# Edge-gated graph kernel: gates ahead of the products in the last nine blocks, early loads moved to GpSimd, and other steps for the row products

## The chip, the cores and the metric

The kernel runs on one core of a Trainium2 chip. The metric is device time in microseconds (us) of one launch; lower is better. Engines are named as in the profile: PE is TensorE (PEld its weight loads), DVE is VectorE, ACT is ScalarE, POOL is GpSimd, SP is SyncE, which here only issues DMAs. Each engine runs its own instructions strictly in the order in which the program lists them; engines wait for each other, and for DMAs, through semaphores.

## The reference

Sixteen graphs share one adjacency matrix `adj` of 1024 x 1024, with some 9 nonzero entries a row. Each of the 1024 nodes has a row of 256 features for each graph. Cut to what matters:

```python
pre_u  = einsum('bud,dk->buk', h, W1[:256])
pre_v  = einsum('bvd,dk->bvk', h, W1[256:])
hidden = relu(pre_u[:, :, None, :] + pre_v[:, None, :, :] + b1)
S   = sigmoid(einsum('buvk,ko->buvo', hidden, W2)[..., 0] + b2)   # a gate for each pair of nodes
a_t = einsum('buv,bud->bvd', S * adj, h)                          # gated sum over neighbours
m_t = einsum('uv,bud->bvd', adj, h) * h                           # plain sum, times h
out = beta1 * h + beta2 * (a_t @ Wa + ba) + beta3 * (m_t @ Wm + bm)
```

A gate is needed only where `adj` is nonzero. The kernel therefore works on a list of edges and never forms the 1024 x 1024 x 256 tensor.

## The kernel before

**Tables, blocks, steps.** The sixteen graphs form four groups of four. For each group there is a table in device memory, with one row for each node: its `pre_u` features for the four graphs and its `h` features for the four graphs (8 KB together). A block is a group with 128 target nodes; there are 32 of them. The first sixteen are six of group 0, six of group 1, then the last two of group 0 and the last two of group 1 (`order`, L408 to L411); the eight of group 2 and the eight of group 3 follow. A block has ten steps (`T`), and a step handles 128 edge slots. Step `n` belongs to block `k = n // 10`, and `s = n % 10` is its place in it; there are 320 steps.

**A step.** `fetch` (L515) is an indirect DMA on POOL that brings the table rows of 128 source nodes into one of eight buffers `fetched`. `expand` (L602) makes `pre_v` of the 128 edges' targets on PE, into one of two PSUM buffers `pc`, from `X`, which holds `pre_v` of the block in split precision. `add` (L637) adds `pc` to `fetched` on DVE. `gate` (L641) is four DVE operations (relu, times W2, sum) with one sum for each graph; then ACT makes the sigmoid (L650) and scales four left-hand matrices by it (L652, tile `left`). `left_adj` (L611) prepares on ACT the left-hand matrices of the next step with the adjacency values. `aggregate` (L655) multiplies `left` by the fetched `h` rows on PE and sums in PSUM (`acc`). When the buffer is used up, the next fetch goes out.

**Products around the steps.** `products` (L800) places the other PE work by step: `halves` makes `X` for the next block (L473: half products at `s` 1 and 3, casts of X on ACT at 4, 6 and 7); `turn_over` (L674) transposes the sums through the PSUM buffers `misc` (there are two) and ACT copies them into `LT` (L685); `block_end` (L701) multiplies `LT` of the block before by `w_a` and `w_m` at `s` 4 to 7, ACT copies each result out of PSUM (L718), and DVE adds it to `h_blk` a step later (L719), from where SP writes it out. `after(step, f)` puts work off to a step, and `do(n)` issues what is due.

**Row products.** The `pre_u` half of the tables is a product too. `rows` (L452) makes it for 128 nodes of a group in two halves: PE multiplies a transposed input tile `hT` by `w_u`, ACT copies the half into a buffer `tab0` or `tab1` (L461, one buffer for each half), and a step later SP writes that buffer to the table (L465). Group 0 is done before step 0 by a `script` (L544), which also builds the first four edge lists. For group 1 the steps are a written plan (L775): for each of its eight tiles the step of the load of `hT` and the steps of the two halves. `made_rows` (L784) carries out the plan, and sends with the load the `h` half of the table (`copy_h`, a DMA on ACT's queue). Table 1 must be complete before step 60 is fetched. The tiles of the plan take two buffers in turn.

**Edge lists.** `lists(vt)` (L242) builds the edge list of 128 target nodes from a row block of `adj`, the key: some sixty small DVE operations, which `fill` slips between the four gate operations of steps. The first four lists are made before step 0. The fifth to eighth start at steps 0, 16, 48 and 88 (`start_list`, L766), first with the key load on POOL (L244), then four steps later with the operations.

**The order within a step.** The order on each engine is written out by hand, in the main loop from L860. Up to step 309: aggregates of earlier steps, `expand(n + 2)`, in step 8 of a block also `do(n)`, then `products(n)`; then `add(n + 1)`, `gate(n)`, `left_adj(n + 1)` and `do(n)`. So ACT has the copies of `products` ahead of the gates of the same step. In the last block the gates come first. At step 1 SP loads `w_a` and `w_m` (L888, L889), which are first used at step 10 (`scale_late`).

Of the kernel before, what the change touches and what calls it, by code (L numbers as in the profile page):

```python
# [13 lines left out]
P = 128  # L14
# [3 lines left out]
def kernel(  # L18
# [42 lines left out]
    nc = tc.nc  # L61
    B, N, D = x.shape
    NT = N // P
    DC = D // P
    GB = 4
# [21 lines left out]
    xT_rows = xT.rearrange("b (c p) n -> p (b c) n", p=P)  # L87
# [6 lines left out]
    def load_weights(src, name, engine=nc.scalar):  # L94
        t = const.tile([P, DC, D], FP, name=name)
        engine.dma_start(t, src.rearrange("(c p) k -> p c k", p=P))
        return t
# [327 lines left out]
        if k in hT_of:  # L425
            hT_free.append(hT_of.pop(k))

    def load_hT(k):
        g, nt = k
        if k in aside_:  # L430
            hTs[k] = hta.tile([P, GB, DC, P], FP, name="hT_")
        else:
            hTs[k] = hT_of[k] = hT_free.pop(0)
        nc.sync.dma_start(hTs[k].rearrange("p b c n -> p (b c) n"),
                          xT_rows[:, g * GB * DC:(g + 1) * GB * DC, nt * P:(nt + 1) * P])

    def copy_h(k, engine=nc.scalar):
        g, nt = k
# [56 lines left out]
    def do(step):  # L495
        for f in due.pop(step, ()):
            f()
# [17 lines left out]
    def fetch(n):  # L515
        k, g, vt, w, j = where(n)
        at_slot[n] = free.pop(0)
        nc.gpsimd.indirect_dma_start(  # L518
            out=fetched[at_slot[n]], out_offset=None, in_=table[g],
            in_offset=bass.IndirectOffsetOnAxis(ap=uidx[:, vt * NW + w, j:j + 1], axis=0),  # L520
            bounds_check=N - 1, oob_is_err=False)
# [19 lines left out]
    for i in range(COPIES):  # L541
        copy_h(turn[i], nc.sync)

    script = ("r r 0 0", "r r 1 0 0", "r r 1", "r 0 0", "r r 1", "0 2 r 1", "0 0 r r", "1 2 r 1", "v r r 2", "r 1 3",  # L544
              "h 2 1 1", "h 2 2 3 u", "2 f 2 2 w h h h", "m 3 w 3 3 3")
    marks, pcs, accs, evs, hbs, LTs, lefts = {}, {}, {}, {}, {}, {}, {}

    def load_mark(q):
# [11 lines left out]
    for t, turns_ in enumerate(script):  # L560
        step = t - 100
        do(step)
        for c in turns_.split():
            if c == "r":
                if m % 2 == 0:
                    piece = rows(turn[m // 2], tabs[m // 2] if m // 2 < len(tabs) else None)
                    next(piece)
                go(piece, step)
                if m % 2 == 0 and m // 2 + COPIES < NT:
                    copy_h(turn[m // 2 + COPIES], nc.sync)  # L570
                m += 1
            elif c == "h":
                go(parts, step)
            elif c == "v":
                fetch_val(T)
                spread(b1_p, b1_b)
                next(parts)
            elif c == "f":
                for n in range(NF):
                    fetch(n)  # L580
            elif c == "u":
                fetch_val(3)
            elif c == "m":
                load_mark(0)
            elif c == "w":
                warm(6)
            else:
                next(made[int(c)], None)
# [174 lines left out]


    advance = {0: (3,), 2: (3,), 4: (3,)}
    start_list = dict(zip((0, 16, 48, 88), range(EARLY, NT)))  # L766
    loads, at = {}, {}

    def plan(blocks, ns):

        for k, (load, *pieces) in zip(blocks, ns):
            loads[load] = k
            at.update((n, k) for n in pieces)

    plan(turn[NT:], ((0, 1, 8), (1, 9, 12), (9, 18, 19), (13, 22, 28), (20, 29, 32), (29, 38, 39), (33, 42, 48), (40, 49, 51)))  # L775
    for g, first in ((2, 60), (3, 140)):
        plan([(g, vt) for vt in range(NT)], ((first - 4 + 10 * i, first + 8 + 10 * i, first + 12 + 10 * i)
                                             for i in range(NT)))
# [4 lines left out]

    def made_rows(n):  # L784
        nonlocal piece, last
        if n in loads:
            if loads[n] in begun and loads[n][0] == 1:
                aside_.remove(loads[n])
            load_hT(loads[n])
            if loads[n] not in begun:  # L790
                copy_h(loads[n])
                begun.add(loads[n])
        if n in at:
            if at[n] != last:
                last = at[n]
                piece = rows(last)
                next(piece)
            go(piece, n)

    def products(n, k, s):  # L800
        nonlocal end, parts
        made_rows(n)
        if (s == 2 and 0 < k < BS) or n == total:
            turn_over(k - 1, 1, 1, n)
        z = 3 if n < ROOM else 4
        if z <= s < z + 4 and 0 < k < BS:
            if s == z:
                end = block_end(k - 1)
                next(end)
            go(end, n)  # L810
        if ROOM <= n < total - T:
            if s in (8, 9):
                turn_over(k, 0, s - 8, n)
        elif s == 7 and k < BS:
            turn_over(k, 0, 0, n)
        if s == 7 and k == BS - 1 or s == 8 and n < ROOM:
            turn_over(k, 0, 1, n)
        if (s == 0 and 0 < k < BS) or n == total - 1:
            turn_over(k - (s == 0), 1, 0, n)
        if n == total - 2:  # L820
            end = tail(tails[:2], n)
            next(end)
        elif n == total - 1:
            go(end, n)
        elif n >= total:
            end = tail([tails[2 + n - total]], n)
            next(end)
            go(end, n)
            go(end, n)
        later = n >= ROOM  # L830
        if k + 1 < BS and s - later in (0, 2, 3, 5, 6):
            if s == later:
                parts = halves(k + 1)
                next(parts)
            go(parts, n)
# [3 lines left out]
    left_adj(0)  # L839
    total = BS * T  # L840
    ROOM, MORE, LISTS = 10, 3, 110
    ahead = NF
    add(0)

# [15 lines left out]
    for n in range(total + 2):  # L860
        k, s = divmod(n, T)
        if n < total - 3:
            last_in = n - 1 if n % 2 or n < ROOM else done
        else:
            last_in = n
        while done < min(last_in, total):
            gather_in(done)
            done += 1
        if n % TW == 1 and n // TW + 1 < total // TW:
            load_mark(n // TW + 1)  # L870
        if n < total - T:
            expand(n + 2)
            if n >= ROOM:
                fill(n, False)
                if s == 8:
                    do(n)
            products(n, k, s)
        if n + 1 < total:
            add(n + 1)
        if n < total:  # L880
            gate(n)
            if n + 1 < total:
                left_adj(n + 1)
        do(n)
        if n >= total - T and n + 2 < total:
            expand(n + 2)
        if n == 1:
            w_a = load_weights(Wa, "w_a", nc.sync)  # L888
            w_m = load_weights(Wm, "w_m", nc.sync)  # L889
            bias = load_rows(bm, D, "bias", nc.sync, spare[:, 1])  # L890
            ba_b = load_rows(ba, D, "ba_b", nc.sync, spare[:, 2])
            be1 = load_rows(beta1, 1, "be1", nc.sync)
            be2 = load_rows(beta2, 1, "be2", nc.sync)
            be3 = load_rows(beta3, 1, "be3", nc.sync)
            after(10, scale_late)
        if s in (5, 7) and k < BS - 1:
            h = s // 7
            hb = big.tile([P, 2, D], FP, name="h_blk", bufs=4)
            hbs.setdefault(k, []).append(hb)
            g, vt = order[k]  # L900
            nc.sync.dma_start(hb.rearrange("p b d -> p (b d)"),
                              table[g][vt * P:(vt + 1) * P, GD + 2 * h * D:GD + (2 * h + 2) * D])
        if n == total - 6:
            hbs[BS - 1] = hT_free.pop(0).rearrange("p b c n -> p b (c n)")
            for v, m, f in tails:
                for h, o in tail_rows(x, v, m, f):
                    nc.sync.dma_start(h, o)
        for i in advance.get(n, ()):
            next(made[i], None)
        if n in start_list:  # L910
            running.append([made[start_list[n]], True, n])
            piece_of(running[-1], n)
        if n < ROOM:
            fill(n, False)
        if n >= total - T:
            products(n, k, s)
        if n == LISTS:
            assert not running and all(next(x, None) is None for x in made)
            lists_done()
            more = main.enter_context(tc.tile_pool(name="more", bufs=1))  # L920
            hT_free.extend(hT_places(more, MORE, NH))
        if n == 120:
            nc.gpsimd.partition_all_reduce(longest, rest, P, bass_isa.ReduceOp.max)
            after(n + 12, count_rest)
# [115 lines left out]
```

## Time and profile before

The median of three runs is 1110.08 us (1110.04 to 1113.46). The profile shows one further execution, of 1097.05 us, and everything from the trace refers to that one.

| | |
|---|---|
| median of the runs | 1110.08 us |
| the profiled execution, its own time | 1097.05 us |
| its span, first to last instruction | 1095.2 us |
| busy: PE, DVE, ACT, POOL | 1029.3, 1020.8, 862.0, 465.5 us |
| DMA | 394.56 MB, 360 GB/s |
| mean granted clock of PE | 0.979 |

By stage, from the trace (busy us of an engine in the stretch):

| stretch, us | what runs | PE | DVE | ACT | POOL | DMA, GB/s |
|---|---|---|---|---|---|---|
| 0 to 60 | group 0 table, four lists | 47.51 | 51.01 | 22.47 | 32.60 | 314 |
| 60 to 160 | first steps, fifth list, group 1 rows | 84.24 | 86.92 | 64.59 | 62.88 | 341 |
| 160 to 360 | the same, sixth and seventh list | 189.80 | 191.01 | 160.70 | 106.58 | 378 |
| 360 to 810 | eighth list, rows of groups 2 and 3 | 444.63 | 430.88 | 386.36 | 177.45 | 391 |
| 810 to 1050 | blocks 23 to 30, no rows any more | 229.57 | 232.06 | 205.79 | 81.81 | 346 |
| 1050 to 1095.2 | last block, tail | 33.59 | 28.91 | 22.09 | 4.15 | 158 |

A line of the timeline reads: start, duration, engine, line, operation, output <- input, shapes, count, and in brackets the idle time of that engine just before, with what ended it. Ends of PE instructions are modelled, so its durations are taken from start to start. An engine that idles where it is not the last to finish costs nothing.

### The profile page before, as it was taken

How to read it: one execution, taken by the hardware profiler on the slowest of the kernel's cores; microseconds unless marked ns; L12 is line 12 of the kernel's file. 1: busy time of each engine (PE TensorE's matmuls, PEld its weight loads, DVE VectorE, ACT ScalarE, POOL GpSimd, SP SyncE). 2: the span in 40 equal slices, each digit the busy share in tenths (PEclk: the TensorE clock that was granted, in tenths of full speed). 3: DMA queues.
4: the chain of work that ended last, by engine and by line, in shares of the span. 5: the costliest groups of instructions: out<-in, count | busy, mean ns of one | idle time of the engine just before them, and what ended most of it. 6: DMA issues, size and time to landing. Idle time of an engine off the chain costs nothing.

```text
span 1095.2 us, 24089 instructions
## 1 busy us (share of the span) xinstructions
PE 1029.3 (94%) x7645; PEld 735.7 (67%) x7645; DVE 1020.8 (93%) x3487; ACT 862.0 (79%) x2616; POOL 465.5 (42%) x453
## 2 busy tenths in 40 slices
PE   7876998998999999999999999999999999999986
PEld 7744766776667767677777777777766666666653
DVE  8878999998999999999999999999999999999994
ACT  3435777786889877888988888888888888888873
POOL 2746676472456324554334333333343332333320
PEclk9887999999999989999999999999999999999999
DMA  9998999999999999999999999999999999999991
GB/s 289 330 399 282 331 361 355 398 377 378 388 356 396 399 391 348 380 392 402 406 401 405 395 409 391 392 395 401 358 384 341 353 340 334 337 347 353 347 328 43
DMA packets 149032, 394.56 MB, mean 360 GB/s; under 512 B 18224, under 2 KB 96048, under 8 KB 112688
## 3 DMA queue, kind: packets, MB, share of 16 engines
q0 software_dynamic: 50240, 300.11, 69.8%
q1 hardware_dynamic: 85360, 79.71, 22.7%
q10 hardware_dynamic: 13296, 13.11, 3.7%
q8 instruction: 63, 1.03, 0.4%
q14 instruction: 73, 0.60, 0.1%
HBM read 396.93 MB, written 50.33 MB: 408 GB/s over the span
## 4 chain that ended last, share of the span: by engine, by line
PE 58%; DVE 17%; ACT 12%; DMA 8%; issue 4%; POOL 0%; DVEq 0%; SPq 0%; ACTq 0%; POOLq 0%
PE misc L713 16%; PE acc L664 14%; PE misc L445 13%; PE pc L607 9%; DVE fetched L647 7%; DVE fetched L639 6%; ACT left L652 3%; PE misc L682 2%; DMA fetched<-table,uidx 2%; PE misc L449 2%; DMA hT<-in_xT_dram 2%; ACT X L489 1%; ACT LT L718 1%; DMA table<-tab 1%; DMA key<-in_adjT_dram 1%
## 5 line engine op out<-in xcount | busy, mean ns | idle before, releaser
L518 POOL DMA_INDIRECT fetched<-table,uidx x320 | 344.9, 1078 | 534.8 <-PE acc L664 361.8
L647 DVE SCALAR_TENSOR_TENSOR fetched<-fetched,w_b 128x256 f32<-128x256 f32 x1280 | 477.1, 419 | 0.0
L639 DVE TENSOR_TENSOR fetched<-fetched,pc 128x1024 f32<-128x1024 f32 x320 | 387.9, 1212 | 11.5 <-PE pc L607 5.0
L652 ACT ACTIVATE left<-left,gt 128x32 f32<-128x32 f32 (+1 forms) x1280 | 299.5, 305 | 10.4
L664 PE MATMUL acc<-fetched,left 128*32 128x256 f32 x4096 | 287.3, 389 | 19.4 <-ACT left L652 19.3
L607 PE MATMUL pc<-X,mark 128*128 128x512 f32 x640 | 244.8, 464 | 16.2 <-DVE fetched L639 14.6
L664 PEld LDWEIGHTS acc<-fetched,left 128*32 128x32 f32 x4096 | 133.9, 110 | 131.9 <-ACT left L652 42.3
L607 PEld LDWEIGHTS pc<-X,mark 128*128 128x128 f32 x640 | 106.0, 191 | 96.4 <-issue 35.4
L650 ACT ACTIVATE gt<-sc,b_b 128x4 f32<-128x4 f32 x320 | 95.9, 300 | 57.9 <-DVE fetched L647 55.1
L713 PE MATMUL misc<-w_m,LT 128*128 128x256 f32 x496 | 117.3, 379 | 0.0
L713 PE MATMUL misc<-w_a,LT 128*128 128x256 f32 x496 | 117.2, 379 | 0.0
L445 PE MATMUL misc<-w_v,hT 128*128 128x256 f32 x448 | 107.6, 384 | 0.0
L713 PEld LDWEIGHTS misc<-w_a,LT 128*128 128x128 f32 x496 | 94.0, 190 | 15.1 <-ACT LT L685 0.4
L713 PEld LDWEIGHTS misc<-w_m,LT 128*128 128x128 f32 x496 | 94.1, 190 | 14.8
L385 POOL DMA_INDIRECT val<-in_adjT_dram,vidx x80 | 89.8, 1122 | 33.6 <-issue 16.1
L617 ACT ACTIVATE left<-onehot,val 128x64 f32<-128x64 bf16 (+1 forms) x320 | 102.9, 322 | 0.0
L647 DVE DVE_READ_ACCUMULATOR fetched<-fetched,w_b 128x1 f32 x1280 | 101.7, 79 | 0.0
L445 PEld LDWEIGHTS misc<-w_v,hT 128*128 128x128 f32 x448 | 86.3, 193 | 13.8
L682 PE MATMUL misc<-ident,ev 128*128 128x128 f32 x512 | 79.8, 279 | 10.8 <-ACT tab L461 5.5
L682 PEld LDWEIGHTS misc<-ident,ev 128*128 128x128 f32 x512 | 61.5, 142 | 37.8 <-ACT ev L672 15.4
L482 ACT CAST X<-misc 128x512 fp32r<-128x512 f32 x64 | 37.3, 583 | 59.8 <-PE misc L445 59.7
L685 ACT COPY LT<-misc 128x512 f32<-128x512 f32 x128 | 73.1, 572 | 7.0 <-PE misc L682 5.9
(178 smaller groups left out, 1006.1 us busy)
## 6 DMA issues: line engine op xcount, KB each, us to landing
h_blk<-table SPq DMA_DIRECT2D x62, 256.0 KB, 9.8
out_dram<-h_blk SPq DMA_DIRECT2D x62, 256.0 KB, 12.6
hT<-in_xT_dram SPq DMA_DIRECT2D x28, 512.0 KB, 20.5
table<-in_x_dram ACTq DMA_DIRECT2D x24, 512.0 KB, 13.8
table<-tab SPq DMA_DIRECT2D x48, 256.0 KB, 11.1
fetched<-table,uidx POOLq DMA_INDIRECT x320
table<-in_x_dram SPq DMA_DIRECT2D x8, 512.0 KB, 11.6
table<-fetched SPq DMA_DIRECT2D x8, 512.0 KB
```

The lines of the kernel that those rows point to most:

```text
L385: nc.gpsimd.indirect_dma_start(out=val[:, i, j:j + 1], out_offset=None, in_=adj_flat, in_offset=bass.IndirectOffsetOnAxis(ap=vidx[:, i, j: ...
L445: nc.tensor.matmul(p[:, bb * D:(bb + 1) * D], hT[:, 2 * h + bb, i, :], wt[:, i, :], start=(i == 0 and not begun), stop=(i == DC - 1), skip ...
L518: nc.gpsimd.indirect_dma_start(out=fetched[at_slot[n]], out_offset=None, in_=table[g], in_offset=bass.IndirectOffsetOnAxis(ap=uidx[:, vt * ...
L607: nc.tensor.matmul(pcs[n][:, c], marks[n // TW][:, j * P:(j + 1) * P], cuts[k][:, w, c], start=True, stop=True)
L617: nc.scalar.activation(lefts[n][:, :m, 1::GB, :], onehot[:, i, o:o + m, :].unsqueeze(2).to_broadcast([P, m, GB // 2, V]), AF.Copy, scale=v ...
L639: nc.vector.tensor_tensor(t, t, pcs.pop(n), ALU.add)
L647: nc.vector.scalar_tensor_tensor(t[:, b, :], t[:, b, :], 0.0, w2_b, ALU.max, ALU.mult, accum_out=sc[:, b:b + 1])
L650: nc.scalar.activation(gt, sc, AF.Sigmoid, bias=b2_b)
L652: nc.scalar.activation(lefts[n][:, :m, 2 * b, :], lefts[n][:, :m, 1 + b // 2 * GB, :], AF.Copy, scale=gt[:, b:b + 1])
L664: nc.tensor.matmul(accs[h][b * 2 * V:(b + 1) * 2 * V, r, :], left[:, i, 2 * b - b % 2:2 * b - b % 2 + 2].rearrange("p k v -> p (k v)"), f[ ...
L682: nc.tensor.transpose(pt[:, r, :, c, :], ev[:, r, c * P:(c + 1) * P], ident)
L713: nc.tensor.matmul(pz[:, bb * D:(bb + 1) * D], LTs[k][:, 2 * h + bb, i if bb else 1 - i, c, :], wt[:, c, :], start=False, stop=(i == 0 and ...
```

## The change

1. **Gates first from block 23 on.** A step `LAST = (BS - NT - 1) * T = 230` takes the place of the start of the last block: from there the gates precede `expand` and `products` of the same step.
2. **Step 8.** In all blocks from step 10 to step 229 the early `do(n)` of step 8 goes, and the first `turn_over` of the block (transposes, ACT's copy into `LT`) moves behind the gates of step 8. In later blocks both are behind the gates through point 1.
3. **Loads on GpSimd.** The second `hT` of group 1, `w_a`, `w_m` and the key of the fifth list are issued by POOL between the eight first fetches: three of them after the third fetch, the key after the sixth. The first `hT` of group 1 is loaded by SP at the end of the script. The `copy_h` DMAs of both tiles go out at steps 1 and 2 (0 and 1 before).
4. **Other steps.** The halves of group 1's row products, their loads, and the starts of the lists get other steps.

```diff
-    def load_hT(k):
+    def load_hT(k, engine=nc.sync):
...
-              "h 2 1 1", "h 2 2 3 u", "2 f 2 2 w h h h", "m 3 w 3 3 3")
+              "h 2 1 1", "h 2 2 3 u", "2 f 2 2 w h h h", "k m 3 w 3 3 3")
...
             elif c == "f":
                 for n in range(NF):
                     fetch(n)
+                    if n == 2:
+                        load_hT(turn[NT + 1], nc.gpsimd)
+                        w_a = load_weights(Wa, "w_a", nc.gpsimd)
+                        w_m = load_weights(Wm, "w_m", nc.gpsimd)
+                    elif n == 5:
+                        next(made[EARLY])
+            elif c == "k":
+                load_hT(turn[NT])
...
-    start_list = dict(zip((0, 16, 48, 88), range(EARLY, NT)))
+    start_list = dict(zip((7, 18, 48, 86), range(EARLY, NT)))
...
-    plan(turn[NT:], ((0, 1, 8), (1, 9, 12), (9, 18, 19), (13, 22, 28), (20, 29, 32), (29, 38, 39), (33, 42, 48), (40, 49, 51)))
+    plan(turn[NT:], ((1, 2, 4), (2, 8, 9), (5, 12, 18), (10, 19, 22), (20, 28, 29), (23, 32, 38), (30, 39, 42), (40, 48, 49)))
...
     def made_rows(n):
         nonlocal piece, last
-        if n in loads:
+        if n in loads and loads[n] in turn[NT:NT + 2] and loads[n] not in begun:
+            copy_h(loads[n])
+            begun.add(loads[n])
+        elif n in loads:
...
         if ROOM <= n < total - T:
-            if s in (8, 9):
+            if s == 9 or s == 8 and n >= LAST:
                 turn_over(k, 0, s - 8, n)
...
+    LAST = (BS - NT - 1) * T
...
-        if n < total - T:
+        if n < LAST:
             expand(n + 2)
             if n >= ROOM:
                 fill(n, False)
-                if s == 8:
-                    do(n)
             products(n, k, s)
...
         do(n)
-        if n >= total - T and n + 2 < total:
+        if s == 8 and ROOM <= n < LAST:
+            turn_over(k, 0, 0, n)
+        if n >= LAST and n + 2 < total:
             expand(n + 2)
         if n == 1:
-            w_a = load_weights(Wa, "w_a", nc.sync)
-            w_m = load_weights(Wm, "w_m", nc.sync)
...
-        if n < ROOM:
+        if n < ROOM or n >= LAST:
             fill(n, False)
-        if n >= total - T:
+        if n >= LAST:
             products(n, k, s)
```

More of the change, by code (lines that the diff above doesn't have):

```diff
@@ L433, in load_hT @@
             hTs[k] = hT_of[k] = hT_free.pop(0)
-        nc.sync.dma_start(hTs[k].rearrange("p b c n -> p (b c) n"),
-                          xT_rows[:, g * GB * DC:(g + 1) * GB * DC, nt * P:(nt + 1) * P])
+        engine.dma_start(hTs[k].rearrange("p b c n -> p (b c) n"),
+                         xT_rows[:, g * GB * DC:(g + 1) * GB * DC, nt * P:(nt + 1) * P])
     def copy_h(k, engine=nc.scalar):
```

## The prediction

> **What bounds the kernel now.** I read the page's slices first, then busy time in windows, then the timelines of the stretches in which an engine falls short. The profiled execution took 1097.05 us (span 1095.2). Windows by stage (us, then busy time of PE, weight load, DVE, ACT, POOL, clock, DMA share, GB/s):
>
> ```profile
> 690.50:720.70 30.20, 30.13 (x239) 21.95 (x234) 28.90 (x98) 26.34 (x83) 11.15 (x10) 1.00 1.02 393
> 870.40:900.30 29.90, 28.60 (x224) 19.61 (x217) 28.90 (x96) 25.64 (x81) 10.22 (x10) 1.00 0.92 345
> ```
>
> The first window is one block in the middle: TensorE is never idle, since it also makes two half row products of 1.73 us each. Blocks 11 to 22 are like that. The second is a block after the last row product (block 23 on): nothing is full. Both PE and DVE miss about 1 us, and the block still takes 29.9. The DVE and PE timelines there show why:
>
> ```profile
> 893.68 0.75 DVE L719 SCALAR_TENSOR_TENSOR h_blk<-h_blk,be,LT 128x512 f32<-128x512 f32 x1 [1.00 <-ACT LT L718]
> ...
> 876.24 1.69 PE L664 MATMUL acc<-fetched,left 128*32 128x256 f32 x16 [0.65 <-ACT left L652]
> ...
> 895.45 1.69 PE L664 MATMUL acc<-fetched,left 128*32 128x256 f32 x16 [0.52 <-ACT left L652]
> ```
>
> DVE stands in front of the addition to h_blk, placed ahead of the gates of step 8, until ACT has copied the product out of PSUM; PE stands because ACT makes its copies first and its gates later. The same three lines recur in every block from 23 to 30.
>
> Then the two large holes, on DVE, ACT and POOL:
>
> ```profile
> 73.43 0.56 POOL L244 DMA_DIRECT2D key<-in_adjT_dram  x1 [2.05 <-DMA fetched<-table,uidx]
> ...
> 86.15 0.69 DVE L252 SCALAR_TENSOR_TENSOR key<-key,ukey 128x512 f32<-128x512 f32 x1 [5.79 <-DMA key<-in_adjT_dram]
> ...
> 89.56 1.65 PE L664 MATMUL acc<-fetched,left 128*32 128x256 f32 x8 [6.13 <-ACT left L652]
> ...
> 256.33 0.58 ACT L461 COPY tab<-misc 128x512 f32<-128x512 f32 x1 [5.18 <-DMA table<-tab]
> 259.81 0.69 DVE L696 TENSOR_TENSOR LT<-LT,hT 128x512 f32<-128x512 f32 x1 [1.26 <-ACT LT L685]
> 262.09 1.22 DVE L639 TENSOR_TENSOR fetched<-fetched,pc 128x1024 f32<-128x1024 f32 x1 [1.58 <-PE pc L607]
> ```
>
> At 80 us DVE, in the gates of step 4, meets the first operation on the fifth key, whose load GpSimd issued only at 73.43, behind eight fetches, and waits 5.79 us; PE follows. At 251 us ACT wants to write the second half of the last row product (step 51) into a buffer whose previous contents (step 48) are still being written to the table, and stands for 5.18 us; DVE loses 1.26 + 1.58 there.
>
> **What the Trainium skill says.** "DMA: Bandwidth & Descriptors", section "Issuing engines are not separate DMA queues": DMAs of all engines run on the same 16 DMA engines and interleave, and another issuer saves only issue time. The trace agrees: from 60 to 80 us the share is 1.02 and the rate 385 to 419 GB/s with three queues in use, so moving hT and weights from SP to GpSimd moves bytes and removes none. The same page, "Anatomy of one DMA", says many descriptors can be emitted before their cost shows. Here 64 rows take POOL a median 0.549 us (L338) and 128 rows 0.585 (L244); 1024 pieces, as in an hT, no row shows. "TensorE: Matmul & The Clock Gate", Part 1: an idle window of about 3.4 us halves the clock. The trace agrees, 0.50 at 65 to 70 us after a pause of 7.13 us, but also has 0.51 at 405 to 410 us after pauses of 0.39, 1.34 and 0.68.
>
> **The change part by part.**
>
> *Fifth key load earlier, its operations later.* The load now stands after the sixth of the eight first fetches, and DVE first uses it in steps 8 and 9 instead of 4. Fetches 1 to 7 landed about 2.6 us apart (66.3, 67.9, 70.6, 73.1 ..., read from the POOL waits 0.3 us before each L338 and L244). Ahead of the key lie six fetches and about 1.05 MB of hT and weights (2.6 us at 400 GB/s), so it lands near 80; step 8 comes at 88. The wait of 5.79 us goes. What is late next: the seventh and eighth fetch, behind 0.5 MB of key (1.3 us), near 80.3 and 83.7. DVE wants them at 83.2 (80.3 plus gates 1.4, low 1.1 and onehot 0.4) and 85.7. The ninth is issued near 76 as before, the tenth near 84 when the eighth has landed. POOL then issues at best a fetch per 3.0 us (2.33 issues of 1.3 us), and DVE needs one per 2.5 to 3.4. That is close. I take 5.0 of 5.8.
>
> *hT, w_a and w_m on GpSimd.* Three more issues in front of the fourth fetch. Cost in POOL time: at least 3 x (0.55 + 0.30) = 2.6 us; at most, if 1536 pieces cost what the 128 rows of an indirect fetch do (0.99 us), 12 us. I take the low end, since 64 more rows cost 0.04. Then the fourth fetch is issued at 60.3 instead of 57.7, still 10 us before it landed, and the ring stays full: nothing. At the high end it lands near 75, 3 us after DVE wants it (71.9). SP is rid of 1.05 MB ahead of its small loads, which can bring the first two fetches forward: up to 1.7 us (DVE's wait at 66.41), not counted. SP's remaining hT load is unchanged in time; the weights are used first at step 10, 108 us.
>
> *Other steps for the row products.* The sixteen halves now stand at steps 2, 4, 8, 9, 12 to 49 instead of 1, 8, 9, 12 to 51. The buffer of each half is reused after 4 steps or more (12 after 8, 22 after 18, 32 after 28, 42 after 38; the last at 48 and 49 after 39 and 42). Gaps of four steps stood before as well, four times, without a wait: L461 waited on a DMA once, after three steps. So the wait at 251 us goes; I count DVE's 2.84 us, as the lists of block 6 keep DVE the bound up to block 7. The hT loads now have seven to nine steps before their products instead of nine (20 us and more, median landing 20.5): a product late by a few us is possible, and not counted. One 1.73 us product less in steps 10 to 51, where PE is nearly full: not counted either. Operations of the fifth list run in steps 8 to 28 and of the sixth in 24 to 44 instead of 24 to 42: moved, not added.
>
> *Addition and transpose of step 8 behind the gates, all blocks.* In blocks 11 to 22 DVE's wait there (0.96 to 1.30 us) goes, but PE is the bound: nothing. In blocks 1 to 10 I count nothing either; PE is full at those places.
>
> *Gates first from block 23.* PE's order does not change; ACT's does, and DVE's addition falls behind the gates. Walk of the block at 870.40: DVE ends the gates of step 7 at 892.6. ACT then needs 0.33 (gate), 0.87 (four lefts), 0.24 (next left) and 0.5 for the copy: 894.6. The addition is due when the gates of step 8 end, 892.6 + 2.51 = 895.1: no wait, with 0.5 us to spare. The lefts of step 7 are there at 893.8 instead of 895.9, and PE wants them at 894.9: its 0.52 goes, and most of the 0.65. The two PSUM buffers named misc come free up to 2 us later: the transpose of step 8 is copied near 897.0 instead of 896.2, and PE takes that buffer at 899.1. PE's own need is a full block less two half products, 30.1 - 3.5 = 26.6, so DVE's 28.9 sets the block. Eight waits (833.87 to 1043.29) of 0.99: 7.9 us. The last block, gates first already, has no DVE wait from step 0 until its tail at 1074.
>
> *Sum:* 5.0 + 2.8 + 7.9 = 15.7 us. Against the profiled execution 1097.05 - 15.7 = 1081.3. The median of the runs shown is 13 us higher, and no view tells where those lie; I take the same difference from it: 1110.1 - 15.7 = 1094.4.
>
> **Rivals.**
>
> *The early gain is given back* (0.17). POOL issues without pause from 126 to 184 us, and DVE waited 2.17 us for a fetch at 154.6; a start that is 5 us earlier may only wait longer there. For it: DMA share near 1. Against: it was only 0.62 at 95 to 105 us. 1110.1 - 10.7 = 1099.4.
>
> *Gates first gives nothing* (0.10): copies of X and of the products come later, PE stands for a misc buffer, or the addition still waits, its margin being 0.5 us. Against: PE has 2.3 us of slack a block. 1110.1 - 7.8 = 1102.3.
>
> *More than counted* (0.08): also the fetch wait of 2.2, the product of 1.7 and 0.8 at the start: 1089.7.
>
> *Slower* (0.11), by the clock: with DVE the bound, PE idles 2.3 us a block in blocks 23 to 30. If that falls into one pause of about 1.3 us, the clock may halve as it did at 405 us, where DVE then waited 3.05 us for pc. Eight of these cost 24.4: 1118.8. It decides from six blocks of eight. Against: pauses of 0.52 and 0.65 left the clock at 1.00.
>
> **How the numbers follow.** The forecast above has the remaining 0.54, its own range 1090 to 1099. Chances: forecast 0.54, given back 0.17, nothing from gates first 0.10, more 0.08, slower 0.11. I hold 0.3% (3.3 us) to be what can be told from no change; both shortfalls together would land in it, so 0.07 of the faster cases goes to the same: faster 0.82, same 0.07, slower 0.11. The range runs from 1086 (the largest gain, with the hidden items) to 1106 (a shortfall with a late hT of some 3 us, or the high end of POOL's cost), leaving out the slow clock.
>
> **What would show it.** Right: no key wait on DVE near 80 us; no L461 wait on a table write; the DVE wait before the h_blk addition gone in blocks 23 to 30, their period 28.9 to 29.1 us, and still 30.1 in blocks 11 to 22. Wrong: a POOL issue of hT well above 0.6 us with DVE waiting for the fourth fetch; waits of DVE on fetches between 85 and 180 us; PE waiting for ACT's X or LT copies, or a clock under 1.00 after block 23.

## The result, and the profile after

The changed kernel takes 1095.26 us (median of six runs), the kernel before 1110.60 in the six runs beside it: ratio 0.9859, 95% interval 0.9835 to 0.9882, so 15.3 us less (13.1 to 18.3). A second set of runs, E5 below, gave 1091.5 against 1112.5, ratio 0.9808 (0.9770 to 0.9845), so 21.0 us less (17.2 to 25.6).

The two first profiles do not show this: the kernel before was profiled in an execution of 1097.05 us, the changed one in one of 1098.79, with spans of 1095.2 and 1097.0. One profile of each is not enough here, and what follows compares stages.

Busy time in two windows of the kernel after, a block with row products and a later one (stretch in us; its length; then busy time of PE, weight load, DVE, ACT, POOL; clock, DMA share, GB/s):

```profile
756.51:786.77 30.26, 30.19 (x235) 22.00 (x234) 29.00 (x97) 26.47 (x82) 10.53 (x11) 1.00 1.01 376
875.66:904.52 28.86, 27.67 (x218) 19.01 (x217) 28.86 (x96) 25.72 (x79) 10.19 (x10) 1.00 0.95 353
```

The first is unchanged, with PE full. In the second DVE is now busy without a gap, 28.86 us of 28.86, where it had 28.90 of 29.90. From the timelines of PE and DVE in that block:

```profile
876.92 0.73 PE L615 MATMUL pc<-X,mark 128*128 128x512 f32 x2 [0.67 <-DVE fetched L647]
878.18 0.66 PE L690 MATMUL misc<-ident,ev 128*128 128x128 f32 x4 [0.53 <-ACT ev L680]
...
903.86 0.74 DVE L727 SCALAR_TENSOR_TENSOR h_blk<-h_blk,be,LT 128x512 f32<-128x512 f32 x1
```

The last line is the addition to `h_blk` of step 8 (L727, L719 before); it carries no wait now. ACT's copy for it ends at 903.44, 0.4 us ahead. PE still idles 1.2 us in the block (1.3 before), with the clock at 1.00: PE has slack and DVE has none.

The start, from the timelines of POOL and DVE of the same execution:

```profile
59.94 0.99 POOL L518 DMA_INDIRECT fetched<-table,uidx  x1 [0.30 <-issue]
60.93 0.98 POOL L434 DMA_DIRECT2D hT__635<-in_xT_dram  x1
61.89 0.78 POOL L96 DMA_DIRECT2D w_a<-in_Wa_dram  x1
62.62 0.76 POOL L96 DMA_DIRECT2D w_m<-in_Wm_dram  x1
63.68 1.06 POOL L518 DMA_INDIRECT fetched<-table,uidx  x1 [0.30 <-issue]
...
92.35 1.22 DVE L647 TENSOR_TENSOR fetched<-fetched,pc 128x1024 f32<-128x1024 f32 x1 [0.70 <-DMA fetched<-table,uidx]
94.87 0.68 DVE L252 SCALAR_TENSOR_TENSOR key<-key,ukey 128x512 f32<-128x512 f32 x1
97.67 1.22 DVE L647 TENSOR_TENSOR fetched<-fetched,pc 128x1024 f32<-128x1024 f32 x1 [2.11 <-DMA fetched<-table,uidx]
...
104.22 1.22 DVE L647 TENSOR_TENSOR fetched<-fetched,pc 128x1024 f32<-128x1024 f32 x1 [3.34 <-remote]
108.83 1.22 DVE L647 TENSOR_TENSOR fetched<-fetched,pc 128x1024 f32<-128x1024 f32 x1 [1.97 <-remote]
```

The three loads cost POOL 0.76 to 0.98 us each, and DVE takes up the fifth key (L252) without waiting. But it stands 8.1 us in four waits before additions, right behind, where the kernel before had none after the key. "Remote" is a releaser that the trace can't name.

### The profile page after: what moved, and what is told of

The parts are those of the page before. It is cut to its first block, busy times and chain, and to the rows that moved or that the text cites. A ratio compares the mean times of both kernels' runs of the same rounds, so it can differ in the third digit from the quotient of the medians.

```text
span 1097.0 us, 24059 instructions
## 1 busy us (share of the span) xinstructions
PE 1027.7 (94%) x7645; PEld 730.7 (67%) x7645; DVE 1022.9 (93%) x3487; ACT 862.6 (79%) x2616; POOL 456.9 (42%) x456
## 4 chain that ended last, share of the span: by engine, by line
PE 53%; DVE 26%; DMA 8%; issue 7%; ACT 4%; SPq 1%; POOL 1%; another core or an unknown queue 0%; ACTq 0%; POOLq 0%; DVEq 0%
PE misc L445 14%; PE acc L672 13%; DVE fetched L655 12%; PE misc L721 11%; DVE fetched L647 10%; PE pc L615 9%; PE misc L690 3%; DMA fetched<-table,uidx 2%; DMA table<-tab 2%; DMA out_dram<-h_blk 2%; PE misc L449 2%; DVE low L484 1%; ACT left L660 1%; DVE LT L704 1%; DVE h_blk L727 1%
## 5 line engine op out<-in xcount | busy, mean ns | idle before, releaser
L518 POOL DMA_INDIRECT fetched<-table,uidx x320 | 338.0, 1056 | 548.4 <-PE acc L672 412.9
L647 DVE TENSOR_TENSOR fetched<-fetched,pc 128x1024 f32<-128x1024 f32 x320 | 387.8, 1212 | 39.4 <-PE pc L615 25.9
L672 PE MATMUL acc<-fetched,left 128*32 128x256 f32 x4096 | 281.6, 385 | 12.0 <-issue 4.6
L672 PEld LDWEIGHTS acc<-fetched,left 128*32 128x32 f32 x4096 | 128.7, 109 | 125.0 <-issue 38.0
L721 PEld LDWEIGHTS misc<-w_a,LT 128*128 128x128 f32 x496 | 93.8, 189 | 15.3 <-issue 0.4
L385 POOL DMA_INDIRECT val<-in_adjT_dram,vidx x80 | 86.3, 1079 | 34.3 <-issue 20.7
L482 ACT CAST X<-misc 128x512 fp32r<-128x512 f32 x64 | 37.1, 579 | 59.3 <-PE misc L445 44.9
L693 ACT COPY LT<-misc 128x512 f32<-128x512 f32 x128 | 72.9, 570 | 11.9 <-PE misc L690 9.1
```

The costliest lines, as they stand in the source:

```text
L385: nc.gpsimd.indirect_dma_start(out=val[:, i, j:j + 1], out_offset=None, in_=adj_flat, in_offset=bass.IndirectOffsetOnAxis(ap=vidx[:, i, j: ...
L518: nc.gpsimd.indirect_dma_start(out=fetched[at_slot[n]], out_offset=None, in_=table[g], in_offset=bass.IndirectOffsetOnAxis(ap=uidx[:, vt * ...
L647: nc.vector.tensor_tensor(t, t, pcs.pop(n), ALU.add)
L672: nc.tensor.matmul(accs[h][b * 2 * V:(b + 1) * 2 * V, r, :], left[:, i, 2 * b - b % 2:2 * b - b % 2 + 2].rearrange("p k v -> p (k v)"), f[ ...
L721: nc.tensor.matmul(pz[:, bb * D:(bb + 1) * D], LTs[k][:, 2 * h + bb, i if bb else 1 - i, c, :], wt[:, c, :], start=False, stop=(i == 0 and ...
```

## The experiments

Twelve runs in three sets (E1 to E4, E5 to E8, E9 to E12); each set has its own chip and its own runs of the kernel before. Each profile was cut at the starts of DVE's 320 additions (L639 before, L647 after), read from its timeline. All times in us:

| profile | first addition | blocks 0 to 10 | 11 to 22 | 23 to 30 | span | ratio to before, interval |
|---|---|---|---|---|---|---|
| before | 63.5 | 381.3 | 362.3 | 239.4 | 1095.2 | |
| E1 before again | 64.9 | 387.3 | 367.0 | 239.3 | 1107.1 | 0.9990 (0.9964 to 1.0016) |
| E2 gates first alone | 66.6 | 380.6 | 366.9 | 230.9 | 1093.8 | 0.9938 (0.9910 to 0.9967) |
| E3 step 8 moved, blocks 1 to 30 | 65.3 | 387.7 | 361.0 | 232.9 | 1096.9 | 0.9890 (0.9843 to 0.9938) |
| E4 start and rows alone | 69.7 | 380.7 | 368.8 | 239.3 | 1108.3 | 0.9922 (0.9893 to 0.9950) |
| after | 67.4 | 381.4 | 368.2 | 231.9 | 1097.0 | 0.9859 (0.9835 to 0.9882) |
| E5 after again | 66.8 | 374.4 | 362.7 | 231.7 | 1084.8 | 0.9808 (0.9770 to 0.9845) |
| E6 step 8 moved, blocks 1 to 22 | 65.1 | 388.6 | 362.2 | 240.7 | 1106.8 | 0.9957 (0.9934 to 0.9980) |
| E7 after, key late | 67.4 | 380.3 | 362.1 | 231.7 | 1090.1 | 0.9835 (0.9799 to 0.9871) |
| E8 after, loads on SP | 64.5 | 385.9 | 364.7 | 231.9 | 1095.6 | 0.9829 (0.9795 to 0.9862) |
| E9 points 1 and 2 alone | 64.4 | 388.9 | 361.8 | 231.8 | 1095.8 | 0.9884 (0.9839 to 0.9929) |
| E10 only the addition moved | 64.8 | 382.7 | 363.5 | 232.8 | 1092.7 | 0.9912 (0.9873 to 0.9951) |
| E11 gates first from block 11 | 65.8 | 377.0 | 366.8 | 230.9 | 1089.1 | 0.9869 (0.9832 to 0.9905) |
| E12 after, old row steps | 69.0 | 378.9 | 360.7 | 231.8 | 1088.9 | 0.9814 (0.9774 to 0.9855) |

Blocks 23 to 30 repeat within 0.2 us among kernels with the same order in blocks 22 to 30 (E6, where block 22 has another order than block 23, takes 1.4 more, all of it in block 23). In blocks 0 to 10 two profiles of one kernel differ by 6 to 7. So the late part is read from single profiles, the early part only from several, and better from the medians of the runs.

**E1: the kernel before, a second profile.** No edit.

> The kernel before, unchanged, for a second profile. Its first profiled execution took 1097.05 us, 13 us under its median. Theory: the 13 us are made of short pauses at places that differ from one execution to the next (waits whose releaser the trace calls remote, PE pauses marked issue, each 1 to 8 us), so that a second profile near 1110 has some 13 us more of them, outside the places that the change touches; the block period in blocks 23 to 30 is 29.9 us again, the key wait near 80 us about 5.8, the table-write wait at step 51 about 5.2. Rival: the 13 us lie in the places that the change touches (longer key wait, longer blocks), so that the change's parts are worth more than the first profile said.

Measured: median 1108.4, profiled at 1108.9. Block 11 starts at 452.2 instead of 444.8 (7.4 us later), and blocks 11 to 22 take 4.7 us more: that is all of the 12 us between the two profiles. The key wait is 5.68 again, blocks 23 to 30 are equal. Neither theory had the middle part: five of its twelve blocks (12, 13, 14, 16, 17) take 30.9 us instead of 30.1, although PE hardly idles in them. They make 3.8 of the 4.7 us; block 11 makes the rest. The timeline of E1 at the start of block 13, weight loads included, shows what differs:

```profile
511.50 0.75 DVE L719 SCALAR_TENSOR_TENSOR h_blk<-h_blk,be,LT 128x512 f32<-128x512 f32 x1 [2.04 <-ACT LT L718]
...
517.54 2.40 PE L664 MATMUL acc<-fetched,left 128*32 128x256 f32 x24
517.56 0.59 ACT L685 COPY LT<-misc 128x512 f32<-128x512 f32 x1 [0.65 <-PE misc L682]
...
518.37 0.90 ACT L652 ACTIVATE left<-left,gt 128x16 f32<-128x16 f32 x4
...
518.73 0.73 PEld L664 LDWEIGHTS acc<-fetched,left 128*32 128x32 f32 x8 [0.60 <-ACT left L652]
```

The same place of the first profile of the kernel before:

```profile
502.44 0.75 DVE L719 SCALAR_TENSOR_TENSOR h_blk<-h_blk,be,LT 128x512 f32<-128x512 f32 x1 [1.29 <-ACT LT L718]
...
507.75 0.58 ACT L685 COPY LT<-misc 128x512 f32<-128x512 f32 x1
...
508.49 1.66 PE L664 MATMUL acc<-fetched,left 128*32 128x256 f32 x24
508.58 0.90 ACT L652 ACTIVATE left<-left,gt 128x16 f32<-128x16 f32 x4
```

In E1 ACT's copy L685 stands 0.65 us for PE's transposes. Behind it in ACT's order are the gate and the `left` of the same step; PE is already inside its aggregate and waits for that `left`. So 24 matmuls take 2.40 us instead of 1.66. The row of PE itself shows no wait: it is inside the group, and only the weight-load row reveals it. In all three profiles with the addition ahead of the gates that have such blocks (E1 five, E2 three, E4 two), each of these blocks has a wait of this copy of 0.60 to 0.73 us at that step. (E2 has also one of 31.7 us, with a wait of 1.45.) With the addition behind the gates the same wait stands in two blocks: 0.65 us in block 12 of E7, where the 24 matmuls took 1.91 us and the block 30.2, and 0.71 in block 13 of E11, which takes 30.6 like its neighbours.

**E2: gates first alone.** The edit, in the kernel before:

```diff
+    LAST = (BS - NT - 1) * T
...
-        if n < total - T:
+        if n < LAST:
             expand(n + 2)
...
-        if n >= total - T:
+        if n >= LAST:
             products(n, k, s)
```

> Theory: gates first from block 23 on, alone, is worth what it was priced at: eight waits of 0.99 us, -7.9 us, about 1102.5; the period of blocks 23 to 30 is 28.9 us and the key wait of about 5.8 us near 80 us stays. Rival 1: it is worth nothing alone, 1110. Rival 2: it carries the whole gain, 1095.

Measured: 0.9938 x 1108 is 6.9 us less (3.7 to 10.0); blocks 23 to 30 take 230.9 instead of 239.3, 8.4 us, at 28.87 us a block. The theory stands; it does not carry the whole gain.

**E3: step 8 behind the gates in all blocks, without gates first.**

```diff
-            if s in (8, 9):
+            if s == 9:
                 turn_over(k, 0, s - 8, n)
...
-                if s == 8:
-                    do(n)
...
         do(n)
+        if s == 8 and ROOM <= n < total - T:
+            turn_over(k, 0, 0, n)
```

> The transpose and addition of step 8 behind the gates in blocks 1 to 30, gates of the other steps where they were. Theory: in blocks 11 to 22 PE is the bound, so nothing there; in blocks 23 to 30 the addition no longer stands ahead of the gates, so the DVE wait of 0.99 us goes there too and most of the gain of the gates first comes from this alone: about -6, 1104, period 29.1 us. Rival: in blocks 23 to 30 it needs the gates first as well (ACT copies the products before its gates), period 29.9 us, 1110.

Measured: 12.2 us less (6.9 to 17.4), twice the expectation. Blocks 23 to 30 give 6.4 of it (29.03 us a block from 24 on), as expected. The rest, for which the interval leaves 0.5 to 11 us, would lie in blocks 1 to 22, which the theory had at nothing; E6 tests that.

**E4: the start and the row products alone**, steps 10 to 319 in the order of before: points 3 and 4 of the diff without the others.

> All of the early part (loads on GpSimd, key after the sixth fetch, other steps for the row products and list starts), and steps 10 to 319 in the order of before. Theory: 5.0 for the key and 2.8 for the table write, -7.8 us, about 1102.5; with the gates-first kernel's gain it sums to the whole of the change (-15.3). Rival 1: the gain is given back in the waits for fetches between 85 and 200 us, 1107 to 1110. Rival 2: it is worth more than counted and the later part less, 1098.

Measured: 8.6 us less (5.5 to 11.9), where the theory had 7.8: the early part as a whole is worth what it was priced at. Its profile can't show that: it was an execution 8 us above its median. Blocks 11 to 22 took 368.8 and the first addition came latest of all, at 69.7.

**E5: the kernel after, a second profile.** No edit.

> The changed kernel, unchanged, for a second profile. In its first profile and in that of the early part alone, ACT stood 5.4 and 7.5 us before a copy of the first table at 34 to 44 us, and the first addition of step 0 came at 67.4 and 69.7 us; in four profiles with the old start it came at 63.5 to 66.6. Theory: that pause is chance (the instructions up to there are the same), so a second profile may have the addition near 65; the blocks 23 to 30 take 231 to 232 us again, blocks 0 to 10 about 381, and the ratio to the kernel before is 0.986. Rival: the new start costs some 3 us, the first addition stands at 67 to 70 again.

Measured: ratio 0.9808 where 0.986 was expected, 21.0 us less. First addition at 66.8, so the rival's 67 to 70 is nearly met. Blocks 0 to 10 took 374.4, 7 us less than in the first profile.

**E6: step 8 moved in blocks 1 to 22 only**: the edit of E3 with `n < 230`.

> The kernel before with only the transpose and addition of step 8 moved behind the gates, and only in blocks 1 to 22. Theory: PE is the bound there, so 0 (1108, ratio 0.997 to 1.003), blocks 11 to 22 in 361 to 368 us as in the kernel before. Rival: it gives the 5 to 6 us by which the kernel with this in all 30 blocks was faster beyond what its blocks 23 to 30 show (ratio 0.995, blocks 11 to 22 at 30.14 us each without the odd longer one).

Measured: 4.8 us less (2.2 to 7.3). The rival holds. Blocks 11 to 22 took 362.2, no less than in the first profile of the kernel before; the two longer ones among them (30.8 us) are without the copy's wait, and the blocks behind them give time back (29.9 and 29.4). E3, E8, E9 and E12 have one or two such blocks as well.

**E7: the kernel after with the key late.**

```diff
-    start_list = dict(zip((7, 18, 48, 86), range(EARLY, NT)))
+    start_list = dict(zip((0, 16, 48, 88), range(EARLY, NT)))
...
-                    elif n == 5:
-                        next(made[EARLY])
```

> The changed kernel with the fifth key's load behind the eight fetches, its operations from step 4, and list starts 0, 16, 48, 88, as before. Theory: the DVE wait for the key near 80 us comes back (5.8 us), +5.0, ratio 0.990 to 0.991. Rival: the waits for fetches that the changed kernel has between 92 and 110 us go in exchange, so that it costs 0 to 2 us, ratio 0.986 to 0.988.

Measured: median 1093.8 against 1091.5 of E5 in the same set, 2.3 us more, with intervals that overlap. From DVE's timeline (lines stand two lower in this kernel):

```profile
88.16 0.69 DVE L252 SCALAR_TENSOR_TENSOR key<-key,ukey 128x512 f32<-128x512 f32 x1 [4.37 <-DMA key<-in_adjT_dram]
...
102.20 1.22 DVE L645 TENSOR_TENSOR fetched<-fetched,pc 128x1024 f32<-128x1024 f32 x1 [0.73 <-remote]
```

The key wait is back, and of the waits that the kernel after has between 92 and 109 us only 0.73 is left. In the stretch from 66 to 112 us DVE stands 5.7 us in all here, 6.1 in E5 and 9.2 in the first profile of after. Block 0 takes 37.9 us against 36.0 (mean of after, E5, E11, E12): the early key is worth about 1.9 there, read from one profile of E7, while that block differs by 1.5 us among the four.

**E8: the loads on SP**, at the same place of the program: `nc.gpsimd` becomes `nc.sync` in the three calls.

> The changed kernel with the second hT, w_a and w_m issued by SP at the same place of the program instead of by GpSimd. Theory: the same bytes pass the same DMA engines, POOL is rid of 2.5 us of issuing ahead of the fourth fetch, which is hidden: 0, ratio 0.986. Rival 1: SP, which has none of the fetches ahead of these loads, sends the 1 MB ahead of the first fetches and delays them, +2 to +4 us. Rival 2: GpSimd's issuing delays the fourth to eighth fetch and so the early steps: -2 us.

Measured: 1094.8 against 1091.5, not distinguishable. The first addition comes at 64.5, as with the old start (mean of seven profiles 64.9), while six profiles with the loads on GpSimd have it at 65.8 to 69.7, mean 67.7. Neither rival had it this way round, and blocks 0 to 10 take 385.9, so the end is the same. That a different issuer buys nothing in the end agrees with the Trainium skill, "DMA: Bandwidth & Descriptors", section "Issuing engines are not separate DMA queues", quoted above.

**E9: points 1 and 2 alone**, the start and row products of before.

> The kernel before with points 1 and 2 of the change (step 8 behind the gates, gates first from block 23), start and row products as before. Theory: 8.4 us in blocks 23 to 30 and about 4 us in blocks 1 to 22, where the extra 0.75 us of many blocks goes (PE inside an aggregate, waiting for a left of ACT): together -12, ratio 0.989, which leaves only some 4 to 8 us to the early part (loads, key, row steps). Rival: the two are not additive, -8, ratio 0.9925, and the early part carries half of the change.

Measured: 12.9 us less (7.9 to 17.8). The theory stands: E2's stage and E6 add up. Together with the 8.6 of E4 this makes 21.5 us, near the 21.0 of E5 and more than the 15.3 of the first set.

**E10: of step 8 only the addition.** Two lines go from the kernel before; what was due is done behind the gates, the transpose stays ahead:

```diff
                 fill(n, False)
-                if s == 8:
-                    do(n)
             products(n, k, s)
```

> Of the step-8 edit only the addition to h_blk: it is made after the gates of step 8, the transpose and ACT's copy stay ahead of the gates, in all blocks. Theory: it is DVE standing before the addition that delays the gates, then ACT's lefts, then PE; so this alone gives the period of 28.9 to 29.1 us in blocks 23 to 30 and takes the blocks of 30.9 us out of blocks 11 to 22: about -10, ratio 0.990. Rival: ACT's copies ahead of its gates are what delays the lefts; the period stays at 29.5 to 29.9 us and the ratio at 0.995 or above.

Measured: 9.8 us less (5.4 to 14.1). Blocks 24 to 30 take 29.02 us each, and no block from 12 on is over 30.5. From its timeline in a late block:

```profile
896.55 0.59 ACT L718 COPY LT<-misc 128x512 f32<-128x512 f32 x1
...
898.03 0.75 DVE L719 SCALAR_TENSOR_TENSOR h_blk<-h_blk,be,LT 128x512 f32<-128x512 f32 x1
...
898.94 1.69 PE L664 MATMUL acc<-fetched,left 128*32 128x256 f32 x16 [0.53 <-ACT left L652]
```

The copy has ended 0.9 us before DVE comes to the addition of step 8. PE's 0.53 for `left` is still there. With the gates first as well it goes, and a block takes 28.87 us instead of 29.02: 0.15 a block for ACT's order. Waits in blocks 11 to 22 as sums (engine, what waited and for whom: us, times, longest), first of E1, then of E10:

```profile
DVE h_blk L719 <- ACT LT L718: 19.4, 12, 2.2
PEld acc L664 <- ACT left L652: 8.6, 19, 1.0
```

```profile
DVE fetched L639 <- PE pc L607: 12.1, 12, 1.2
...
PEld acc L664 <- ACT left L652: 4.2, 12, 0.6
```

DVE still waits once a block, now before the addition of `pc` of step 1 and for PE, which is the bound. PE's weight loads wait half as long for `left` as in E1 (5.4 us in the first profile of the kernel before, which has no long blocks).

**E11: gates first from block 11 on**: `LAST = 11 * T` in the kernel after.

> The changed kernel with the gates first from block 11 on instead of 23. Theory: in blocks 11 to 22 PE is the bound, 30.14 us a block, and the gates first make ACT's copies of X and of the row products later, which PE waits for through the two misc buffers: no gain, blocks of 30.14 us or up to 0.7 longer, ratio 0.986 to 0.993. Rival: it takes the last short waits of PE for lefts (4.2 us of weight loads in that stage) and gains 2 to 4 us, ratio 0.978 to 0.982.

Measured: blocks 12 to 22 take 30.5 to 30.6 us, all of them, 0.4 more than with PE full. The waits in that stage name it:

```profile
PEld misc L690 <- ACT low L483: 13.2, 12, 1.7
...
PE misc L690 <- ACT low L483: 8.4, 12, 1.3
```

ACT comes to its two copies of a half product of X (L482, L483) only after its gates, and PE stands for the `misc` buffer, once a block. So moving DVE's addition back paid in both stages, with PE full (E6) and with PE slack (E10), while moving ACT's gates forward costs time where PE is full.

**E12: the kernel after with the old steps of the row products** from the third tile on.

```diff
-(2, 8, 9), (5, 12, 18), (10, 19, 22), (20, 28, 29), (23, 32, 38), (30, 39, 42), (40, 48, 49)
+(2, 8, 9), (9, 18, 19), (13, 22, 28), (20, 29, 32), (29, 38, 39), (33, 42, 48), (40, 49, 51)
```

> The changed kernel with the third to eighth row product of group 1 at their old steps (halves at 18, 19, 22, 28, 29, 32, 38, 39, 42, 48, 49, 51). Theory: ACT's wait for the table write before step 51 comes back, some 5 us on ACT near 255 us and 2.8 on DVE: +2.8 us, ratio 0.984 to 0.989. Rival: blocks 4 and 5 are bound by DVE and the fetches, and the wait is absorbed: 0.

Measured: 0.9814, not slower than either set of the kernel after. ACT's timeline:

```profile
196.26 0.58 ACT L461 COPY tab<-misc 128x512 f32<-128x512 f32 x1 [2.96 <-DMA table<-tab]
...
252.12 0.56 ACT L461 COPY tab<-misc 128x512 f32<-128x512 f32 x1
...
262.49 0.59 ACT L461 COPY tab<-misc 128x512 f32<-128x512 f32 x1
```

The last two lines are steps 48 and 51, which write the same buffer. The wait of 5.18 us for the table write before step 51 was to come back: it isn't there. Among the eight profiles with the old steps it is in four: 5.18 us in the first profile of the kernel before, 1.3 to 1.7 in E2, E3 and E9. In the six with the new steps no copy of the last tile waits for a write. The first line is another wait, at step 32, four steps after the buffer was used last; the prediction took four steps to be enough. Over the fourteen profiles further waits of L461 for a write (named, or remote) behind the start sit at 104, 158, 416 and 577 us in one or two profiles each. One recurs in nine, with old and new steps alike: 1.9 to 6.1 us at step 29 (181 to 191 us), for a releaser that the trace can't name. The one at 577 us is in the first profile of the kernel after alone, and it is why that has 368.2 us in blocks 11 to 22:

```profile
576.80 0.58 ACT L461 COPY tab<-misc 128x512 f32<-128x512 f32 x1 [5.01 <-DMA table<-tab]
...
577.44 1.00 PE L690 MATMUL misc<-ident,ev 128*128 128x128 f32 x4 [3.74 <-ACT tab L461]
```

No variant is shown to be faster than the kernel after; E12 may be as fast.

## Why the prediction was right, and where not

The time was 1094.4 forecast, 1095.26 measured, and the gain 15.7 against 15.3. That the numbers meet so closely is in part luck: the second set measured 21.0, and one term of the sum, put at nothing, is worth 4.8 by E6. By stage, with means over the profiles of the table:

| stage | forecast | measured | from |
|---|---|---|---|
| start to block 11 | 7.8 | 4.5 | 450.2 (seven old starts, 444.8 to 453.7) to 445.8 (E4, after, E5, E11, 441.3 to 450.4) |
| blocks 11 to 22 | 0 | 3.3 | 366.3 (before, E1, E2, E4) to 363.0 (nine with the addition behind the gates, E11 left out) |
| blocks 23 to 30 | 7.9 | 7.5 | 239.3 to 231.8 (after, E5, E9) |

The last row is firm. The two others are not: the profiles behind each mean differ by 6 to 9 us in them, and single pauses of some 5 us (block 11 of E4, block 15 of the first profile of after) are included. The medians of the runs give 8.6 (5.5 to 11.9) for the early part (E4) and 4.8 (2.2 to 7.3) for step 8 in blocks 1 to 22 (E6). So the early 7.8 is not shown to be wrong as a whole; which of its pieces carry it is another matter, below.

*Gates first from block 23*: the mechanism and the size are right (28.86 us a block; 28.9 to 29.1 said), with no DVE wait before the addition. What carries it is the place of the addition, as E10 shows: 6.5 of the 7.5 us come with that alone. ACT's order adds 0.15 a block, so "ACT makes its copies first and its gates later" was the smaller cause.

*Step 8 in blocks 1 to 22, "PE is the bound: nothing"*: this step failed. E6 measured 4.8 us. The step was read from a block of the one profile, and that execution had none of the blocks of 30.9 us that E1, E2 and E4 have. PE was the bound there with a margin that other executions use up. In the long blocks PE stands inside its aggregate for a `left` behind ACT's copy (E1); with only the addition moved (E10) no block from 12 on is that long. That DVE's wait before the addition makes gates and `left` late enough for ACT's copy to matter fits this, and the copy waits of E7 and E11, but it was not measured step by step. The long blocks make 3.8 us in E1, as much in E2, 1.4 in E4 and nothing in the first profile, less on average than the 4.8 of E6; blocks 0 to 10 show no gain in the profiles (382.7 to 388.9 in E3, E6, E9 and E10, 380.6 to 387.3 in before, E1 and E2). Where the rest lies, if it is one, stays open.

*"The median of the runs shown is 13 us higher, and no view tells where those lie; I take the same difference from it"*: a second profile tells. 7.4 of E1's 12 us lie before block 11 and 3.8 in the long blocks, which go when the addition is moved. The difference could not be carried over whole.

*Fifth key, "I take 5.0 of 5.8"*: the term was too large, as far as E7 shows. The wait went, as said, but the fetches were late next, as the rival "given back" and the sign "waits of DVE on fetches between 85 and 180 us" had it: some 1.9 us is left by block 0 of E7, and 2.3 by its median, whose interval overlaps that of E5. The ninth and tenth fetch were issued at 80.28 and 88.22 instead of the 76 and 84 reckoned with.

*Other steps, 2.8 for the table write*: E12 finds nothing. The wait of step 51 comes with the old steps, but in half of their profiles only and mostly at 1.3 to 1.7 us; 5.18 belonged to one execution. The sign "no L461 wait on a table write" was not met either: the first profile of after has one of 5.01 us, at 577. With the key at some 2 us and these steps at nothing, most of the 8.6 us of E4 has no piece to its name. The earlier loads of `hT` and weights and the steps of the first two row products were not tested alone.

*Loads on GpSimd, low end*: right. Without them the fourth fetch could have been issued 0.30 us after the third ended, at 61.23; it was issued at 63.68, so they cost 2.45 us against the 2.6 reckoned. What was not foreseen is the later first addition, by 2.7 us on average with these loads on GpSimd. The first fetch is already late by then (57.07 instead of 53.73 in the first profiles), behind ACT's wait of 5.43 us at 40 us for an unnamed releaser and a wait of DVE for ACT of 6.7 us; up to there the instructions are the same. That DVE wait is 4.8 to 5.8 us in six of the seven profiles with the old start (the first profile has none) and 5.4 to 10.2 in the six with these loads. Whether the change or chance makes it is open.

*Slower by the clock*: blocks 23 to 30 of the first profile of after all show a clock of 1.00. PE idles 1.2 us a block there, in pauses of 0.53 and 0.67, and not the 2.3 reckoned.

## What to carry to other kernels

Put an operation that waits for another engine behind work that engine's consumers need, even in a stage where a third engine seems to be the bound (here 4.8 us with PE full): the profiled execution may have had a margin that others use up. Before pricing a stall from one profile, ask whether the profiled execution agrees with the median; if it is 13 us off, take the stalls that recur in every block and discount those that occur once. At this start, with the DMA engines near full, a wait that was taken away came back in part one transfer later.

## What was not expected of the hardware

ACT's copy L685 waits 0.60 to 0.73 us for PE in some blocks and not at all in others, with the same instructions and with all its neighbours at the same distances (in E1 everything up to it lies 9.05 us after the first profile's). Why the same transposes are reported later there was not settled.

PE lost 0.7 us inside one group of matmuls while its own row names no wait: the group is longer (2.40 instead of 1.66 us for 24), and the weight-load row has the wait of 0.60.

Two executions of one kernel differ by 7 us in blocks 0 to 10 (after: 381.4 and 374.4), where the DMA share is 1.00. Most of the waits for table writes and fetches move from one place to another there.
